# Turning the rows of the later steps by DMA over 16-bit planes in a GRU, ternary layer and mixture-of-experts kernel

## The chip, the cores and the metric

The kernel runs on one core of a Trainium2 chip. The metric is the device time of one launch in microseconds (us), lower is better; it is given as the median of several runs. The engines are called TensorE (PE in the profile; its weight loads are PEld), VectorE (DVE), ScalarE (ACT), GpSimd (POOL) and SyncE (SP, which issues DMAs). SBUF is the on-chip memory of 128 partitions, PSUM the accumulators that TensorE writes to.

## The reference, cut to what matters

The input is 128 sequences of 64 steps of 512 values (x: 128 x 64 x 512, float32) and a start state for each sequence (cond: 128 x 512). What is computed:

```
# block 0
h = cond
for t in 0..63:                       # GRU cell
    gi, gh = x[:, t] @ W_ih + b_ih, h @ W_hh + b_hh
    r = sigmoid(gi_r + gh_r);  z = sigmoid(gi_z + gh_z)
    n = tanh(gi_n + r * gh_n)
    h = (1 - z) * n + z * h
    hs[:, t] = h
x = x + hs @ ternary(weight).T * scale + bias
# block 1
c = causal depthwise convolution of x along the steps, 128 taps a channel = cond, + b
scores = softmax(c @ gate_w.T)        # 64 experts, the best 6 of each token
y = sum over the token's experts, at most 64 tokens an expert:
        score * (silu(c @ w_gate[e]) * (c @ w_up[e])) @ w_down[e]
x = x + y + (silu(c @ sw_gate) * (c @ sw_up)) @ sw_down      # the shared expert
```

The tokens are the 8192 pairs of sequence and step. The change touches the part between the convolution and the shared expert, and the very first loads.

## The kernel before

**Stages.** In the trace of before the GRU runs from 0 to about 1217 us, the convolution to about 1280, the shared expert with the routing (scores and the choice of the six experts) from 1280 to about 1758 as blocks i = 0 to 7, and the routed experts, with the other half of the shared expert's blocks laid among them, from there to the end. The program is written as one Python function for a framework that orders the instructions of each engine by itself from their dependencies; each engine then runs its own list in order, and waits at an instruction until what it needs is there. Where the program says `tc.issue_after` or `behind`, the order is set by hand.

**Rows and turned rows.** The convolution leaves its result in SBUF as `hid(t)`, one tile of 128 x 512 float32 for each of the 64 steps: 128 sequences on the partitions, 512 values along them. The tiles of the steps 0 to 31 and 32 to 63 are two buffers. The products need the 512 values on the partitions instead. So each step is *turned*: `turn(t)` (L1117 to L1129) transposes its four 128 x 128 parts on TensorE into one bank of PSUM (`pst`, L1128), and VectorE copies that bank back over `hid(t)` (L1138). Before that the rows, as they are, go to the table `tab` in device memory (`put_rows`, L1232, SP's queue), from which the routed experts later gather them. The turned rows of the steps from 32 on are also stored to `xts` (L1144, SP's queue), because the memory of `hid` is given to the experts' weights after block 7; they come back by the load at L1293.

**Blocks and routing.** A block is four steps (NB = 4), so there are NI = 16, and block i has steps 4i to 4i + 3. The loop `for i in range(NI // 2)` handles blocks 0 to 7 of the shared expert by `shared(i)`, a generator of 44 pieces, and draws from a second generator, `routing`, between the pieces. While block i's shared expert runs, `route` turns and scores blocks 2i + 1 and 2i + 2: eight turns at the start (one for each piece drawn), one group of logits (`lg`, L1152), and then for each of the two blocks the softmax, the score store to `tab` (L1196, SP's queue, two DMAs), and the choice of the best six. The tile `sc` that holds the scores is one buffer: the second block's scores overwrite the first's.

**The shared expert in a block.** Five chunks of seven products each (`winograd`, L824, into the banks psx, psw, psz and y), then two halves of the down product. A bank is one buffer (y has two), so TensorE goes on with a bank only when ScalarE or VectorE has taken its content out (L853 to L871); the evictions come one to three products before the bank is needed again. Sums of parts of the block's rows are kept in the memory of block i - 2 (`sums_space`), whose steps are done with by then.

**Finished blocks.** A finished block's rows are added to the output by four accumulating DMAs on GpSimd's queue (`add_shared`, L1106).

**The start.** Loads on SP's queue: the turned input of step 0 (`load_xt`, L256, 256 KB), then the GRU's input weights in halves of 512 KB (`load_halves` calls `load_rows`, L108). TensorE does some warm-up matmuls (L326) and then the first product (psy<-rawi,xp, L336).

Of the kernel before, what the change touches and what calls it, by code (L numbers as in the profile page):

```python
# [9 lines left out]
BF16 = mybir.dt.bfloat16  # L10
I32 = mybir.dt.int32
U8 = mybir.dt.uint8
F32R = mybir.dt.float32r
AF = mybir.ActivationFunctionType
ALU = mybir.AluOpType
# [4 lines left out]
P = 128  # L20
B = 128
T = 64
D = 512
# [24 lines left out]
def adaln_ffn_kernel(  # L48
# [57 lines left out]
    def load_rows(dst, src):  # L106

        return nc.sync.dma_start(out=dst, in_=src.rearrange("(k p) n -> p k n", p=P))  # L108
# [102 lines left out]
    with (  # L211
# [79 lines left out]
        def repeated(dst, row):  # L291
            nc.sync.dma_start(out=dst, in_=row.partition_broadcast(P))

        def load_halves(dst, src):
            for k in range(2):
                load_rows(dst[:, k * HK : (k + 1) * HK], src[k * HD : (k + 1) * HD])

        h = el0.tile([P, D], F32, name="h")
        bh = {0: io0.tile([P, D], F32, name="xn"), 1: el0.tile([P, D], F32, name="n")}

        load_xt(0, nc.sync)
        load_halves(raw_i[0], w_ih[:, cols[0]])
        load_halves(raw_i[2], w_ih[:, cols[2]])
        nc.sync.dma_start(out=h, in_=cond)
        load_xt(1, nc.sync)
        load_halves(raw_i[1], w_ih[:, cols[1]])
        load_rows(raw_h[0], w_hh[:, cols[0]])
        repeated(br, b_ih[cols[0]])
        repeated(bh[0], b_hh[cols[0]])
# [365 lines left out]
    def hid(t):  # L675
        return hids[t // TH][:, t % TH, :]
# [432 lines left out]
    with (  # L1109
        tc.tile_pool(name="sm", bufs=1) as sm,  # L1110
        tc.tile_pool(name="ps_t1", bufs=2, space=PSUM) as ps_t1,
        tc.tile_pool(name="ps_l", bufs=1, space=PSUM) as ps_l,
    ):

        sc = sm.tile([P, NB, NE + 2], F32, name="sc")  # L1117
        nc.gpsimd.memset(sc[:, :, NE:], -1.0)

        def turn(t):  # L1120

            if t in (2, 3):
                ps = ps_y.tile([P, D], F32, name="y")
            else:
                ps = ps_t1.tile([P, D], F32, name="pst1")
            ps = ps.rearrange("p (k b) -> p k b", k=KD)
            for k in range(KD):
                last = nc.tensor.transpose(ps[:, k, :], hid(t)[:, k * P : (k + 1) * P], ident)  # L1128
            return ps, last  # L1129

        def route(its, turned={}):


            for i in its:
                for t in range(i * NB, i * NB + NB):
                    ps = turned[t] if t in turned else turn(t)[0]
                    with behind(marks, t in turned):
                        copied = nc.vector.tensor_copy(  # L1138
                            hid(t).rearrange("p (k b) -> p k b", k=KD), ps
                        )  # L1140
                    if t == NB - 1:
                        marks.append(copied)
                    if t >= TH:
                        nc.sync.dma_start(out=xts[t - TH], in_=hid(t))  # L1144
                    yield


            lg = ps_l.tile([P, 2, 2, P], F32, name="lg")
            for n, i in enumerate(its):
                for k in range(KD):  # L1150
                    for h_ in range(2):
                        nc.tensor.matmul(  # L1152
                            lg[h_ * NE : (h_ + 1) * NE, n],
                            gw[:, k, :],
                            rows_of(i)[:, 2 * h_ : 2 * h_ + 2, k * P : (k + 1) * P],
                            start=(k == 0),
                            stop=(k == KD - 1),
                        )

            def logits(n):  # L1160
                ls = sh.tile([P, QT], F32, name="g2").rearrange("p (j b) -> p j b", j=2)
                nc.scalar.copy(ls, lg[:, n])
                return ls

            ls = logits(0)
            yield
            for n, i in enumerate(its):
                if len(its) == 1:
                    lgT = ps_l.tile([P, 2, 2, P], F32, name="lg")[:, 0]
                else:  # L1170
                    lgT = ps_t1.tile([P, D], F32, name="pst1")[:, :QT].rearrange(
                        "p (j b) -> p j b", j=2
                    )
                for j in range(2):
                    nc.tensor.transpose(lgT[:, j], ls[:, j, :], ident)

                lgT = lgT.rearrange("p j (h e) -> p (j h) e", h=2)
                nmax = sm.tile([P, NB], F32, name="nmax")
                nc.vector.tensor_reduce(nmax, lgT, AX.X, ALU.max)
                scn = sc[:, :, :NE]  # L1180
                nc.vector.tensor_tensor(
                    scn, lgT, nmax.unsqueeze(2).to_broadcast([P, NB, NE]), ALU.subtract
                )
                nc.scalar.activation(scn, scn, AF.Exp)
                yield
                ssum = sm.tile([P, NB], F32, name="ssum")
                nc.vector.tensor_reduce(ssum, scn, AX.X, ALU.add)
                nc.vector.reciprocal(ssum, ssum)
                nc.vector.tensor_tensor(
                    scn, scn, ssum.unsqueeze(2).to_broadcast([P, NB, NE]), ALU.mult  # L1190
                )
                yield
                top = sm.tile([P, NB, 8], F32, name="top")
                rep = sm.tile([P, NB, NE + 2], F32, name="rep")
                for a in range(2):
                    nc.sync.dma_start(  # L1196
                        out=tab_t[i * NB + 2 * a : i * NB + 2 * a + 2, :, D:].rearrange(
                            "t b e -> b t e"
                        ),
                        in_=sc[:, a::2, :NE],  # L1200
                    )
                for r in range(NB):
                    nc.vector.max(top[:, r], sc[:, r, :NE])
                nc.vector.memset(top[:, :, TOPK:], -1.0)
                if n + 1 < len(its):
                    ls = logits(n + 1)
                yield
                for j in range(NB):
                    t, r = i * NB + j, 2 * (j % 2) + j // 2
                    nc.vector.match_replace(rep[:, r], top[:, r], sc[:, r], -5.0)  # L1210
                    if t == 0:
                        nc.vector.tensor_scalar(
                            cum[:, t, :], rep[:, r, :NE], -5.0, None, ALU.is_equal
                        )
                    else:
                        nc.vector.scalar_tensor_tensor(
                            cum[:, t, :],
                            rep[:, r, :NE],
                            -5.0,
                            cum[:, t - 1, :],  # L1220
                            ALU.is_equal,
                            ALU.add,
                        )
                    if j % 2:
                        yield

        def put_rows(i):
            if i < NI:

                with tc.issue_after(loaded.ins):  # L1230
                    for t in range(i * NB, i * NB + NB):
                        (nc.gpsimd if i == 1 else nc.sync).dma_start(  # L1232
                            out=tab_t[t, :, :D], in_=hid(t)
                        )


        for i in range(1, 3):
            put_rows(i)
        load_rows(swd, sw_down[: full * P, :])
        for j in range(2):  # L1240
            nc.sync.dma_start(out=swdr[j * rest : (j + 1) * rest, :], in_=sw_down[full * P :, :])

        ahead = route([0])
        for _ in range(NB):
            next(ahead)

        with tc.issue_after(marks[-1].ins):
            marks.append(prepare_shared(0))
        second = {}
        for t in (NB, NB + 1):  # L1250
            second[t], last = turn(t)
        with tc.issue_after(last.ins):
            next(ahead)
        for i in range(NI // 2):
            put_rows(2 * i + 3)
            put_rows(2 * i + 4)

            def routing():
                if i == 0:
                    yield from ahead  # L1260
                its = [r for r in (2 * i + 1, 2 * i + 2) if r < NI]
                yield from route(its, second if i == 0 else {})

            routing_ = routing()
            done = 0
            for n, _ in enumerate(shared(i)):
                if done * PIECES <= n * 20:
                    with behind(products or marks, i == 0):
                        next(routing_, None)
                    done += 1  # L1270
            for _ in routing_:
                pass
            add_shared(i)
    first.close()
# [390 lines left out]
```

## Time and profile before

| what | value |
|---|---|
| median of 3 runs | 2451.47 us (2448.66 to 2453.61) |
| the profiled execution | 2452.42 us, span 2450.7 us |
| TensorE busy | 2436.9 us, 99% of the span |
| VectorE, ScalarE, GpSimd busy | 1546.5, 463.1, 445.8 us |
| start of the blocks 3, 4, 5, 6, 7, 8 of the shared expert | 1467.5, 1527.0, 1586.5, 1646.0, 1705.5, 1761.6 us |
| in block 4 (59.5 us): TensorE, VectorE, ScalarE, GpSimd busy | 59.5, 37.56, 14.37, 3.46 us |
| turns on TensorE | 64 steps, four transposes each |
| mean granted clock of TensorE | 0.999 |

All times are in us from the start of the span unless they are marked ns. In a line of a timeline the columns are start, duration, engine, source line, operation, written tile <- read tiles, shapes and count, and in brackets the idle time before it and what ended it. Durations of instructions that follow each other on one engine overlap a little, so that the distance of two starts, called the pitch here, is what an instruction costs its engine. SPq and POOLq stand for the queues that issue DMAs; a DMA lands when its data is there.

### The profile page before, as it was taken

What the parts mean: (1) busy time and instruction counts of PE and PEld (TensorE: products, weight loads), DVE (VectorE), ACT (ScalarE), POOL (GpSimd) and SP (SyncE); (2) the same over time, 40 slices, a digit from 0 to 9 for tenths busy, and PEclk for the clock granted to TensorE, in tenths of its full rate; (3) what the DMA queues carried; (4) which work ended last, traced back from release to release, by engine and by line L of the source; (5) the groups of instructions that cost most, each with busy time, mean ns of one, the idle gap of its engine ahead of it and who ended that gap; (6) DMA issues with size and microseconds to landing.
All of it is one profiled execution on the core that took longest, in us unless ns stands there. A gap on an engine that the chain in (4) does not pass through costs nothing.

```text
span 2450.7 us, 32124 instructions
## 1 busy us (share of the span) xinstructions
PE 2436.9 (99%) x12317; PEld 1883.7 (77%) x12317; DVE 1546.5 (63%) x3073; ACT 463.1 (19%) x847; POOL 445.8 (18%) x468
## 2 busy tenths in 40 slices
PE   9999999999999999999999999999999999999999
PEld 5888888888888888888896688888876666666667
DVE  8877777777777776777686566666653433343344
ACT  5211111111111111111122222222211111111111
POOL 1122221122112112211220000000012222222220
PEclk9999999999999999999999999999999999999999
DMA  5244443333232223222497112222468999899962
GB/s 183 68 95 81 82 80 63 61 69 65 56 61 56 56 56 62 56 52 52 142 343 270 24 23 44 62 59 61 116 174 287 300 290 312 267 330 293 283 175 52
DMA packets 464456, 322.33 MB, mean 132 GB/s; under 512 B 316592, under 2 KB 384176, under 8 KB 462128
## 3 DMA queue, kind: packets, MB, share of 16 engines
q1 hardware_dynamic: 435408, 246.34, 35.6%
q0 software_dynamic: 28896, 73.95, 13.5%
q8 instruction: 97, 1.59, 0.3%
q14 instruction: 55, 0.45, 0.1%
HBM read 233.44 MB, written 92.03 MB: 133 GB/s over the span
## 4 chain that ended last, share of the span: by engine, by line
PE 98%; DMA 1%; DVE 0%; issue 0%; ACT 0%; SPq 0%; POOL 0%; DVEq 0%; ACTq 0%
PE psa L336 9%; PE psx L336 9%; PE psw L336 9%; PE psx L824 8%; PE psw L824 8%; PE psz L824 8%; PE psy L336 5%; PE psb L336 5%; PE psz L336 5%; PE psf L336 5%; PE y L824 4%; PE py L1550 3%; PE pg L1524 3%; PE pu L1524 3%; PE y L1001 2%; PE psc L193 2%
## 5 line engine op out<-in xcount | busy, mean ns | idle before, releaser
L1534 DVE SCALAR_TENSOR_TENSOR a<-a,rw,pu 128x352 f32<-128x352 f32 x32 | 18.6, 580 | 213.4 <-PE pu L1524 213.4
L354 DVE SCALAR_TENSOR_TENSOR xs<-xl,xcut 128x512 fp32r<-128x512 f32 x63 | 103.6, 1644 | 66.0 <-POOL xl L353 66.0
L347 DVE TENSOR_SCALAR hcut<-pst 128x512 int32<-128x512 int32 x63 | 43.5, 691 | 129.8 <-PE pst L419 127.6
L1106 POOL DMA_DIRECT2D out_dram<-hid x32 | 27.7, 1006 | 449.6 <-issue 333.5
L353 POOL TENSOR_TENSOR xl<-xp,xcut 128x512 fp32r<-128x512 f32 x60 | 82.8, 1380 | 145.2 <-PE psa L336 145.1
L488 ACT ACTIVATE rz<-rz 128x512 f32<-128x512 f32 x64 | 40.5, 633 | 336.1 <-DVE rz L487 336.1
L433 ACT CAST hh<-hcut 128x512 fp32r<-128x512 f32 x61 | 37.9, 622 | 325.0 <-DVE hcut L347 325.0
L271 POOL DMA_DIRECT2D q<-in_x_dram x36 | 19.3, 537 | 409.7 <-DMA out_dram<-q 313.4
L1550 PE MATMUL py<-wd,aeT 128*64 128x512 f32 (+1 forms) x384 | 88.8, 597 | 0.0
L1524 PE MATMUL pg<-wg,xeT 128*64 128x352 f32 x512 | 81.2, 459 | 0.0
L1524 PE MATMUL pu<-wu,xeT 128*64 128x352 f32 x512 | 81.2, 459 | 0.0
L1561 POOL DMA_INDIRECT out_dram<-ys,idxp x32 | 47.0, 1469 | 183.4 <-DMA out_dram<-ys,idxo 103.7
L1561 POOL DMA_INDIRECT out_dram<-ys,idxo x32 | 45.0, 1407 | 174.3 <-DMA out_dram<-ys,idxp 168.1
L336 PE MATMUL psa<-wih1h,xh 128*128 128x512 f32 x252 | 74.5, 416 | 0.0
L271 POOL DMA_DIRECT2D xn<-in_x_dram x28 | 15.0, 536 | 319.1 <-DMA out_dram<-xn 258.3
L1524 PEld LDWEIGHTS pg<-wg,xeT 128*64 128x64 f32 x512 | 36.3, 136 | 47.4 <-issue 47.4
L864 ACT ACTIVATE g<-psx 128x256 f32<-128x256 f32 x80 | 30.7, 384 | 217.5 <-DVE aT L871 158.5
L501 ACT ACTIVATE n<-n 128x512 f32<-128x512 f32 x64 | 40.5, 633 | 163.3 <-DVE n L500 160.9
L336 PE MATMUL psw<-wih2h,xh 128*128 128x512 f32 x252 | 68.7, 394 | 0.0
L336 PE MATMUL psw<-wih2l,xl 128*128 128x512 f32 x252 | 68.5, 392 | 0.0
L336 PE MATMUL psa<-wih1l,xl 128*128 128x512 f32 x252 | 68.2, 392 | 0.0
L336 PE MATMUL psb<-wih1s,xs 128*128 128x512 f32 x252 | 68.1, 392 | 0.0
(429 smaller groups left out, 6170.2 us busy)
## 6 DMA issues: line engine op xcount, KB each, us to landing
wg<-in_w_gate_dram SPq DMA_DIRECT2D x64, 704.0 KB, 12.5
wu<-in_w_up_dram SPq DMA_DIRECT2D x64, 704.0 KB, 12.8
wd<-in_w_down_dram SPq DMA_DIRECT2D x64, 512.0 KB, 10.5
xc<-x1c SPq DMA_DIRECT2D x32, 512.0 KB, 6.8
xp<-in_xT_dram POOLq DMA_DIRECT2D x62, 256.0 KB, 2.9
tab<-hid SPq DMA_DIRECT2D x56, 256.0 KB, 4.3
wd<-in_w_down_dram SPq DMA_DIRECT2D x64, 192.0 KB, 10.7
q<-in_x_dram POOLq DMA_DIRECT2D x36, 256.0 KB, 2.9
```

Source lines behind the costliest of these rows:

```text
L193: i = nc.tensor.matmul(ps[rows, j].rearrange("p h (u t) -> p h u t", u=2), xcs[sl % NCB][:, rows, g * 4 + j], tzs[sl % NCB][:, :, :, g * 4 ...
L336: i = nc.tensor.matmul(ps, lhs[:, k, :], rhs[:, k, :], start=start and k == 0, stop=stop and k == KD - 1, skip_group_check=True,)
L347: return nc.vector.tensor_scalar(dst.bitcast(I32), src.bitcast(I32), LOW, None, ALU.bitwise_and)
L353: i = engine.tensor_sub(lo, full, cut)
L354: nc.vector.scalar_tensor_tensor(mix, lo.bitcast(F32), -SPLIT, cut, ALU.mult, ALU.add)
L488: nc.scalar.activation(r, r, AF.Sigmoid)
L501: nc.scalar.activation(n, n, AF.Tanh)
L824: i = nc.tensor.matmul(ps.rearrange("p (j b) -> p j b", b=P) if len(r.shape) == 3 else ps, lhs(k), r, start=(first and k == 0), stop=(k == ...
L1001: nc.tensor.matmul(gu.rearrange("p (j b) -> p j b", b=P), swr[:, k].rearrange("p w n -> p (w n)"), rows[:, k], start=(k == 0), stop=(k == ...
L1524: nc.tensor.matmul(acc[halves[j]], self.xeT[:, k, halves[j]], self.ws[j][which][:, k, :], start=(k == 0), stop=(k == KD - 1),)
L1550: nc.tensor.matmul(py[halves[j]], self.aeT[:n, c, halves[j]], self.ws[j][2][:n, c, :], start=(c == 0), stop=(c == len(ech) - 1),)
L1561: nc.gpsimd.indirect_dma_start(out=out, out_offset=bass.IndirectOffsetOnAxis(ap=(idxp[:CAP] if j == 0 else idxo)[:, q : q + 1], axis=0), i ...
```

## The change

Three edits.

The steps from 36 on (blocks 9 to 15) are no longer turned by TensorE. In their place a new generator, `turn_away(i)`, runs beside the shared expert's blocks from i = 3 on and turns the steps of the blocks 2i + 3 and 2i + 4, one block of the loop earlier than `route` needs them. For each step ScalarE copies the lower and the upper 16 bits of the 512 words into two planes in a flat buffer (two copies), a transposing DMA on SP's queue turns both planes at once into a second buffer (eight 128 x 128 parts of 16-bit elements), and VectorE copies the two turned planes back over `hid(t)`, each into its half of the words (two copies, two steps later in program order: LAG). These are the four portions of a step, one to each piece of the shared expert. The buffers are the tiles of steps 0 to 7, whose content is no longer needed: two flat and three turned ones for i = 3, three and five after that. `route` then skips its turns for these blocks and begins with the logits.

For the same steps the stores to `xts` go to GpSimd's queue, and so do the score stores of the blocks from 9 on.

At the start, the input of step 0 is loaded on ScalarE's queue, and the first block of the GRU's input weights in four quarters instead of two halves.

```diff
-        load_xt(0, nc.sync)
-        load_halves(raw_i[0], w_ih[:, cols[0]])
-        load_halves(raw_i[2], w_ih[:, cols[2]])
+        load_xt(0, nc.scalar)
+        load_parts(raw_i[0], w_ih[:, cols[0]], KD)
+        load_parts(raw_i[2], w_ih[:, cols[2]])
...
+        AWAY = 3
+        LAG = 2
+        def plane(t, n):
+            return hid(t).bitcast(U16)[:, n * D : (n + 1) * D]
+        def word_halves(t):
+            return hid(t).bitcast(U16).rearrange("p (d h) -> p d h", h=2)
+        def turn_away(i):
+            steps = [
+                t for r in (2 * i + 3, 2 * i + 4) if r < NI for t in range(r * NB, r * NB + NB)
+            ]
+            flat_at, turned_at = (
+                ((0, 1), (2, 3, 7)) if i == AWAY else ((0, 1, 2), (3, 4, 5, 6, 7))
+            )
+            for n in range(len(steps) + LAG if steps else 0):
+                for w in range(2):
+                    if n < len(steps):
+                        at = flat_at[n % len(flat_at)]
+                        nc.scalar.copy(plane(at, w), word_halves(steps[n])[:, :, w])
+                        if w:
+                            nc.sync.dma_start_transpose(
+                                out=hid(turned_at[n % len(turned_at)])
+                                .bitcast(U16)
+                                .rearrange("p (m b) -> p m b", b=P),
+                                in_=hid(at).bitcast(U16),
+                            )
+                    yield
+                    if n >= LAG:
+                        t, at = steps[n - LAG], turned_at[(n - LAG) % len(turned_at)]
+                        nc.vector.tensor_copy(word_halves(t)[:, :, w], plane(at, w))
+                        if w and t >= TH:
+                            nc.gpsimd.dma_start(out=xts[t - TH], in_=hid(t))
+                    yield
...
         def route(its, turned={}):
-            for i in its:
+            apart = its[0] > 2 * AWAY + 2
+            for i in its if not apart else ():
...
-                    nc.sync.dma_start(
+                    (nc.gpsimd if apart else nc.sync).dma_start(
                         out=tab_t[i * NB + 2 * a : i * NB + 2 * a + 2, :, D:].rearrange(
...
+            turning = turn_away(i) if i >= AWAY else iter(())
             done = 0
             for n, _ in enumerate(shared(i)):
                 if done * PIECES <= n * 20:
                     with behind(products or marks, i == 0):
                         next(routing_, None)
                     done += 1
+                next(turning, None)
             for _ in routing_:
+                pass
+            for _ in turning:
                 pass
             add_shared(i)
```

More of the change, by code (lines that the diff above doesn't have):

```diff
@@ L12 @@
 U8 = mybir.dt.uint8
+U16 = mybir.dt.uint16
 F32R = mybir.dt.float32r
@@ L292, in repeated, with load_parts @@
             nc.sync.dma_start(out=dst, in_=row.partition_broadcast(P))
-        def load_halves(dst, src):
-            for k in range(2):
-                load_rows(dst[:, k * HK : (k + 1) * HK], src[k * HD : (k + 1) * HD])
+        def load_parts(dst, src, n=2):
+            for k in range(n):
+                load_rows(
+                    dst[:, k * KD // n : (k + 1) * KD // n], src[k * D // n : (k + 1) * D // n]
+                )
         h = el0.tile([P, D], F32, name="h")
         bh = {0: io0.tile([P, D], F32, name="xn"), 1: el0.tile([P, D], F32, name="n")}
-        load_xt(0, nc.sync)
-        load_halves(raw_i[0], w_ih[:, cols[0]])
-        load_halves(raw_i[2], w_ih[:, cols[2]])
+        load_xt(0, nc.scalar)
+        load_parts(raw_i[0], w_ih[:, cols[0]], KD)
+        load_parts(raw_i[2], w_ih[:, cols[2]])
         nc.sync.dma_start(out=h, in_=cond)
         load_xt(1, nc.sync)
-        load_halves(raw_i[1], w_ih[:, cols[1]])
+        load_parts(raw_i[1], w_ih[:, cols[1]])
         load_rows(raw_h[0], w_hh[:, cols[0]])
@@ L1129, in turn @@
             return ps, last
+        AWAY = 3
[22 more added lines that the diff above has]
+                                in_=hid(at).bitcast(U16),
+                            )
+                    yield
[5 more added lines that the diff above has]
+                    yield
         def route(its, turned={}):
-            for i in its:
+            apart = its[0] > 2 * AWAY + 2
+            for i in its if not apart else ():
                 for t in range(i * NB, i * NB + NB):
```

## The prediction

> **What bounds the kernel now.** I read the page's busy shares and chain first. Times below come from one profiled execution: 2452.42 us for a span of 2450.7, that is 0.95 above the median of 2451.47; differences are summed against the span and then taken from the median.
>
> ```profile
> PE 2436.9 (99%) x12317; PEld 1883.7 (77%) x12317; DVE 1546.5 (63%) x3073; ACT 463.1 (19%) x847; POOL 445.8 (18%) x468
> ...
> PE 98%; DMA 1%; DVE 0%; issue 0%; ACT 0%; SPq 0%; POOL 0%; DVEq 0%; ACTq 0%
> ```
>
> TensorE is the path: what it no longer does is worth its full pitch, as long as no other engine, VectorE first, comes late. The timeline of TensorE at the start of the shared block i = 5 prices the work removed:
>
> ```profile
> 1590.02 0.60 PE L1128 MATMUL pst<-ident,hid 128*128 128x128 f32 x4
> 1590.46 1.03 PE L824 MATMUL psx<-hid,sw0first 128*128 128x256 f32 x4
> ...
> 1593.05 0.60 PE L1128 MATMUL pst<-ident,hid 128*128 128x128 f32 x4
> 1593.49 1.03 PE L824 MATMUL psx<-hid,sw0first 128*128 128x256 f32 x4
> ```
>
> Start to start, one step's turn costs 0.44 us (the next one 0.43). Then the windows. The changed kernel's compiled order (order only, no times) puts the new copies and turns into two stretches. The first 12 steps stand from the end of block i = 2's gate part to early in block 3, which is 1448 to 1484 in this trace. The last 16 stand from the end of block 3's gate part to the second chunk of block 4, 1507 to 1541; 10 or 11 of these cluster at the seam, 1511 to 1532. Columns: PE, PEld, DVE, ACT, POOL busy, clock, DMA share, GB/s.
>
> ```profile
> 1448.00:1484.00 36.00, 36.00 (x176) 29.20 (x175) 23.16 (x65) 6.17 (x14) 3.46 (x4) 1.00 0.26 41
> 1507.00:1541.00 34.00, 34.00 (x166) 27.41 (x165) 21.69 (x64) 6.29 (x13) 3.47 (x4) 1.00 0.33 66
> 1511.00:1532.00 21.00, 21.00 (x97) 15.99 (x96) 11.58 (x38) 2.03 (x5) 3.47 (x4) 1.00 0.35 48
> ```
>
> TensorE is full in all three; VectorE has 12.8, 12.3 and 9.4 us free, ScalarE 29.8, 27.7 and 19.0. Last, the DMA issues (KB each, median us from issue to landing), as no turn by DMA stands in this trace:
>
> ```profile
> x1c<-q SPq DMA_DIRECT2D x36, 256.0 KB, 4.5
> ...
> xts<-hid SPq DMA_DIRECT2D x32, 256.0 KB, 2.0
> ...
> tab<-sc SPq DMA_DIRECT2D x32, 64.0 KB, 1.7
> ...
> tab<-xl POOLq DMA_DIRECT2D x4, 32.0 KB, 5.8
> ```
>
> **The change, part by part.**
>
> *Removed: 28 turns on TensorE* (steps 36 to 63; blocks 4, 5 and 6 lose eight each, block 7 four). 28 x 0.435 = 12.2 us, all on the path. VectorE also loses 28 copies out of PSUM (L1138, 0.69 each, 19.3 us), but in blocks 4 to 7, mostly after the stretches that fill up.
>
> *Added on ScalarE: 56 plane copies* of 128x512. The row for such a copy is 0.62 (xh<-xcut, L377): 24 in the first stretch are 14.9 us against 29.8 free, 32 in the second 19.8 against 27.7. Priced at nothing; the cover is ScalarE's idle time. Were it gone, an eviction would wait one copy, 0.62, and the first reads of psx have some 2 us (the products that lie between) to spare.
>
> *Added on VectorE: 56 word copies*, 16-bit, reading rows and writing every second half word. No such copy is in the trace. Bounds: the SBUF-to-SBUF pass xcut<-xp, 0.42 for 128x512, pitch 0.38; and the copy out of PSUM, 0.69. I take 0.38, because source and destination both lie in SBUF as in xcut. At the seam 23 of them stand between the same neighbours: 23 x 0.38 = 8.7 of 9.4 free us. VectorE just fits, with nothing to spare.
>
> *Added: 28 turns on SP's queue, and waits on them.* ScalarE waits for a turn before it refills that flat buffer (two buffers for the first eight steps, then three), VectorE before the word copies; both run in order, so the evictions that TensorE needs are queued behind. What counts is landing time L against the distance the order leaves. I laid the compiled orders of all engines side by side with row durations (done for before, this gives 60.1 us for a block, the profile 59.5). Example: between the third turn's issue and its word copy VectorE has the three sums of 128x512 that open a block, pitch 0.72, so 2.2 us. ScalarE's distances are often shorter, but it has idle time to absorb its waits; VectorE's are below 2.9 in some 18 of the 28, mostly between 2.2 and 2.8. So L up to about 2.6 costs nothing, and past that about 18 turns each push the path by the excess: 18 x (L - 2.6).
> L is bounded by xts<-hid, 2.0 (same tiles, same size, same queue, same blocks) and x1c<-q, 4.5 (the same bytes in 4096 pieces of 64). The compiled turn works in tiles of 16 rows by 128 16-bit elements, so 256-byte pieces, 1024 of them; tab<-sc moves 256 such pieces in 1.7. By pieces between those two: 1.7 + 768/3840 x 2.8 = 2.3. Turns often issue in pairs, and behind another one waits 0.66 (the pitch of 27 row stores in 17.81 us on SP), half the time: 0.3; a wait sees a landing 0.1 late. L = 2.7, cost 1.8, rounded to 2.0. A gain is excluded: a wait frees nothing.
>
> The Trainium skill speaks against the change: VectorE: DVE Perf Modes, The three transpose paths, puts a 128x128 16-bit transpose at 390 ns on TensorE and 1309 ns by crossbar DMA, and advises TensorE where PSUM will do. Eight such blocks in sequence would be an estimated 10.5 us a step, and the sum would end near 2580 (18 x 7.9 in place of 2.0). DMA: Bandwidth & Descriptors, Latency and other measured facts, gives an effective 261 GB/s for such DMAs, an estimated 1.0 us for 256 KB, which would leave the sum as it is; no run here shows either yet.
>
> *Moved: 28 row stores (xts) to GpSimd's queue.* GpSimd pays 0.87 each (L1106), 24.4 us, and is busy 3.46 of 59.5 per block; their reader (the row load at 1720) is far off. Nothing. They stand ahead of the add stores, which have a block's time.
>
> *Moved: 14 score stores to GpSimd's queue.* VectorE must not overwrite the scores before they are read out: in block 3 they are ready at 1500.70, and the next write starts at 1506.33, 5.6 us later. Two issues, 0.87 each, and a landing of 5.8 (tab<-xl) make up to 6.7, so 1.1 late, in the three blocks with two halves. Bounds 0 (SP's 1.7 fits) and 3.3; I take 1.0, since VectorE has slack again by then. Behind that write stand the evictions of the chunk.
>
> *SP's queue.* The turns pass nothing urgent: the row stores are issued by 1341, weights only from 1721. Block 3's own score stores stand behind turns; they have 5.6 us for 1.7.
>
> *The first block in quarters, xp on ScalarE's queue.* TensorE idles 0.90 at 4.48, until the first half (512 KB) lands 4.0 after its issue:
>
> ```profile
> 1.26 3.99 DMA rawi<-in_w_ih_dram
> 5.25 0.14 issue
> 5.38 6.11 PE psy L336 x8
> ```
>
> A 256 KB quarter, issued first, lands before the warm-up matmuls end (2.9 for xp<-in_xT), so 0.9 goes. Bounds 0 (the four quarters share the engines, DMA 92% busy) to 3.3 (TensorE's passes run at a pitch of 0.86 until about 10.2, then at 0.43; were they at 0.43 from 5.4 on, 2.4 more would go). I take 0.9, the idle row itself.
>
> Sum: -12.2 - 0.9 + 2.0 + 1.0 = -10.1; 2451.47 - 10.1 = 2441.4.
>
> **The rivals.** A measurement of this kernel tells some 0.2%, 4.9 us, from no change.
>
> *A, the forecast:* L below 3.0, word copies near 0.38. 2437 (no waits, start gain kept whole, -14) to 2446.5. For it: xts<-hid at 2.0 in the same place, DMA share only 0.25 to 0.35. Chance 0.56.
>
> *B, the gain is eaten:* word copies at 0.69: the seam needs 11.58 + 23 x 0.69 = 27.5 of 21 us, so 6.5 late: 2441.4 + 6.5 = 2447.9; or L of 3.0 to 3.5, 5 to 14 instead of 2. The time lands within 4.9 of before, 2446.6 to 2456.4. For it: the seam has under 1 us free. Against: SBUF-to-SBUF rows are 0.42. Chance 0.20.
>
> *C, slower: the turn's landing.* At the seam and in the first stretch VectorE stands in order behind turns. With L = 4.5, as x1c<-q, 18 x 1.9 = 34.2 instead of 2.0: 2441.4 + 32.2 = 2473.6. It decides from 2.6 + 12.1/18 = 3.3 on (break-even), and passes 0.2% at 3.5. For it: tab<-hid, whole rows of the same tiles, took a median of 4.3 with many in flight; the turns also come many at a time. Against: the ring of three buffers never has more than three in flight. Chance 0.22.
>
> *D, the DMA does not turn in pieces* but element by element: 435408 packets took 35.6% of 16 engines' 2450.7 us, 32 ns each; 131072 elements are 262 us a step on 16 engines, and 28 steps end near 9.8 ms. Against: the compiled turn names 16x128 tiles. Chance 0.02.
>
> **How the numbers follow.** Faster is A, 0.56; same is B, 0.20; slower is C and D, 0.24. The time is A's, 2441.4. The range runs from 2437 (0.04 of A below) to C with L = 4.1: 18 x 1.5 = 27, so 2466; C's upper part and D, 0.14, are beyond. A alone has 2437 to 2446.5.
>
> **What would show it.** Right: no turn on TensorE from block 4 on; blocks 4 to 6 near 56 us, block 3 and 4 perhaps 1 or 2 more; turns landing in 2 to 3 us; VectorE's waits on them under 5 us in all; first product near 4.5. Wrong: VectorE or ScalarE waiting on hid turns for tens of us with TensorE behind (C); word copies of 0.69 and VectorE full from 1511 on (B); a turn that holds its queue for 5 us or more.

## The result, and the profile after

The changed kernel takes 2473.11 us (median of 4 runs, 2472.34 to 2474.9) against 2451.81 of the kernel before beside it: a ratio of 1.0089, 95% interval 1.0072 to 1.0107, or 21.3 us more. The forecast was 2441.4. The time is near that of rival C, 2473.6. The profiled execution took 2474.9 us, its span 2473.2.

The page of the changed kernel, busy shares and chain of waits:

```profile
PE 2432.5 (98%) x12205; PEld 1875.8 (76%) x12205; DVE 1545.4 (62%) x3101; ACT 493.7 (20%) x903; POOL 475.6 (19%) x510
...
PE 93%; DMA 4%; DVE 1%; ACT 0%; issue 0%; POOL 0%; SPq 0%; DVEq 0%; ACTq 0%; POOLq 0%
```

TensorE runs 112 instructions fewer (28 turns of 4) and saves only 4.4 us of busy time. The chain, 98% TensorE before, now has 4% of DMA in it. The answer for the line that issues the turns (L1159) says which DMA; the numbers after the colon are ns of the issue, min/median/max, the last ones us to landing:

```profile
L1159 SPq DMA_TRANSPOSE hid<-hid x28: 1232/1271/3949, 1449.9 to 1577.6; - x28
...
  ACT hid L1157: 55.0, 18
  DVE hid L1168: 44.9, 15
...
DMA to landing us min/median/max: 3.0/4.8/7.8
```

A turn lands 4.8 us after its issue, never under 3.0, where the sum had 2.7. ScalarE stood 55.0 us before turns, which I had priced at nothing, and VectorE 44.9, where I had written "under 5 us in all". The blocks' windows, cut at their first product (L1004; columns as in the prediction), blocks i = 2 to 5:

```profile
1405.55:1467.32 61.77, 59.76 (x306) 48.36 (x305) 37.51 (x114) 19.40 (x37) 4.56 (x6) 1.00 0.24 43
1467.32:1546.63 79.31, 65.40 (x307) 50.79 (x305) 46.01 (x141) 30.52 (x58) 12.26 (x18) 0.91 0.58 118
1546.63:1618.19 71.56, 60.79 (x274) 46.97 (x272) 40.13 (x130) 24.32 (x47) 14.05 (x21) 0.90 0.56 109
1618.19:1674.15 55.96, 55.96 (x274) 45.34 (x273) 32.56 (x106) 14.44 (x29) 6.41 (x8) 1.00 0.16 24
```

Block 5 is what was hoped for: 55.96 us against 59.50, 3.54 for eight turns, 0.44 each. Blocks 2, 3 and 4 should have been 59.5, 59.5 and 56.0 and are 61.8, 79.3 and 71.6, a loss of 37.7 us. 26.7 of it is TensorE idle (2.0, 13.9 and 10.8, length less busy time). The rest is TensorE busy for longer with the same work, 5.9 us more in block 3 and 4.8 in block 4. The clock column says why: 0.91 and 0.90. The timelines of VectorE and ScalarE around 1485, and under them that of TensorE from 1477 to 1492, show both parts (in brackets the idle time ahead and what ended it):

```profile
1484.34 1.50 DVE L1168 COPY hid<-hid 128x512 uint16<-128x512 uint16 x4 [6.04 <-DMA hid<-hid]
1485.73 0.41 DVE L858 TENSOR_TENSOR u<-u,y 128x256 f32<-128x256 f32 x1
```
```profile
1484.32 0.62 ACT L1157 COPY hid<-hid 128x512 uint16<-128x512 uint16 x1 [6.25 <-DMA hid<-hid]
1484.85 0.36 ACT L856 COPY u<-psx 128x256 f32<-128x256 f32 x1
```
```profile
1477.75 2.07 PE L827 MATMUL psw<-hid,sw1first 128*128 128x256 f32 x4 [4.57 <-DVE hid L1026]
...
1485.26 2.07 PE L827 MATMUL psx<-hid,sw0first 128*128 128x256 f32 x4 [4.58 <-ACT u L856]
1487.13 1.91 PE L827 MATMUL psw<-hid,st 128*128 128x256 f32 x4
...
1491.07 1.03 PE L827 MATMUL psx<-hid,sw 128*128 128x256 f32 x4
```

VectorE stands 6.04 us before word copies; behind them in its list is the eviction L858 that TensorE's banks wait for, and on ScalarE, after 6.25 us, the eviction L856 stands behind a plane copy in the same way. After the idle stretch four matmuls take 2.07 in place of 1.03, until about 1491. The waits of TensorE, in us, times and longest, say whom it waited for in the three blocks:

```profile
PE psx L827 <- ACT u L856: 9.0, 2, 4.6
...
PE pst L1217 <- ACT g L1204: 4.8, 1, 4.8
PE psw L827 <- DVE hid L1026: 4.6, 1, 4.6
```

All in all TensorE stood 14.0 us behind ScalarE and 12.7 behind VectorE, the 26.7 of above.

### The profile page after: what moved, and what is told of

Read it like the earlier page. It is cut to its first block, busy times and chain, and to the rows that moved or that the text cites. A ratio compares the mean times of both kernels' runs of the same rounds, so it can differ in the third digit from the quotient of the medians.

```text
span 2473.2 us, 32065 instructions
## 1 busy us (share of the span) xinstructions
PE 2432.5 (98%) x12205; PEld 1875.8 (76%) x12205; DVE 1545.4 (62%) x3101; ACT 493.7 (20%) x903; POOL 475.6 (19%) x510
## 3 DMA queue, kind: packets, MB, share of 16 engines
q0 software_dynamic: 31584, 82.21, 13.7%
## 4 chain that ended last, share of the span: by engine, by line
PE 93%; DMA 4%; DVE 1%; ACT 0%; issue 0%; POOL 0%; SPq 0%; DVEq 0%; ACTq 0%; POOLq 0%
PE psa L339 9%; PE psw L339 9%; PE psx L339 9%; PE psx L827 7%; PE psz L827 7%; PE psw L827 7%; PE psb L339 5%; PE psz L339 5%; PE psf L339 5%; PE psy L339 5%; PE y L827 4%; PE py L1596 3%; PE pg L1570 3%; PE pu L1570 3%; DMA hid<-hid 3%; PE y L1004 2%
## 5 line engine op out<-in xcount | busy, mean ns | idle before, releaser
L272 POOL DMA_DIRECT2D xn<-in_x_dram x28 | 15.1, 538 | 319.1 <-DMA out_dram<-xn 266.2
L858 DVE TENSOR_TENSOR u<-u,y 128x256 f32<-128x256 f32 x80 | 33.5, 419 | 61.0 <-PE y L827 58.9
L339 PE MATMUL psy<-wih0s,xs 128*128 128x512 f32 x252 | 68.2, 392 | 0.5 <-DVE rz L487 0.5
## 6 DMA issues: line engine op xcount, KB each, us to landing
wd<-in_w_down_dram SPq DMA_DIRECT2D x64, 192.0 KB, 10.5
```

Of the source, the lines that this page charges most:

```text
L339: i = nc.tensor.matmul(ps, lhs[:, k, :], rhs[:, k, :], start=start and k == 0, stop=stop and k == KD - 1, skip_group_check=True,)
```

## The experiments

**Theory landing:** a turn takes longer to land than the compiled order leaves between its issue and the copies that need it, and evictions are queued behind those copies. **Rivals:** the copies' work itself; GpSimd's queue, which got the row stores; turns that land late only because of crowding. In the comparisons below the floor is before less 14.5: 12.2 for the turns and 2.3 for the start; what lies above it is called the loss. By that measure the changed kernel's loss is 35.8.

**The start alone**, on the kernel before:

```diff
-        load_xt(0, nc.sync)
-        load_halves(raw_i[0], w_ih[:, cols[0]])
+        load_xt(0, nc.scalar)
+        load_parts(raw_i[0], w_ih[:, cols[0]], KD)
```

> The kernel before with the start's edit alone (first loads on ScalarE's queue, first block of input weights in four quarters). Between the two profiles the first block of the shared expert began 2.3 us earlier after the change (1282.7 against 1285.0), and nothing but the start had changed up to there. If that is the start's worth, this kernel takes 2.3 us less than before, some 2449. The prediction had put it at 0.9, so 2450.6. Were it 0, the 2.3 would come from the difference between two executions.

2449.85 against 2452.14: 2.3 us less, ratio 0.9992 (0.9983 to 1.0001), so the size is as expected though the interval just touches no change. Little of it is the idle row that I priced: the first product starts at 4.92 in this run's profile and at 5.12 in that of the changed kernel, instead of 5.38, as it now waits for xp on ScalarE's queue. The rest comes along with differences of the clock. TensorE's window from 41.1 to 47.8, first of the kernel before, then of the changed one, then of this run:

```profile
41.10:47.80 6.70, 6.03 (x9) 2.52 (x8) 4.65 (x10) 3.81 (x7) 0.55 (x1) 0.50 0.33 97
```
```profile
41.10:47.80 6.70, 6.38 (x20) 3.14 (x19) 6.70 (x14) 4.77 (x9) 0.56 (x1) 1.00 0.29 96
```
```profile
41.10:47.80 6.70, 6.70 (x16) 3.26 (x15) 5.45 (x12) 3.67 (x7) 0.56 (x1) 0.84 0.32 98
```

Before, TensorE ran there at a granted clock of 0.50 and did 9 instructions; in the changed kernel it has 1.00 and does 20, and the pass psy<-rawh,xn takes 3.60 us after 6.52. In this run, with the same start as the changed kernel, the clock was at 0.50 from 39.83 to 43.24, and the pass takes 4.23; its very first pass, psy<-rawi,xp, takes 4.07 us where it took 6.11 before and 5.78 in the changed kernel. So two profiles of the same start save the time in different places. What in the edit keeps the clock up longer is not shown.

**A plain DMA in place of the turn:**

```diff
-                            nc.sync.dma_start_transpose(
-                                out=hid(turned_at[n % len(turned_at)]).bitcast(U16).rearrange("p (m b) -> p m b", b=P),
-                                in_=hid(at).bitcast(U16),
-                            )
+                            nc.sync.dma_start(out=hid(turned_at[n % len(turned_at)]).bitcast(U16),
+                                              in_=hid(at).bitcast(U16))
```

> The changed kernel with a plain DMA of the same 256 KB from the flat buffer to the second one in place of each turning DMA, on the same queue (the rows of the steps from 36 on stay unturned). All copies by ScalarE and VectorE, all row, score and add stores stay, and the order is nearly the same. Theory landing: the time is lost because a turn lands 4.8 us (median) after its issue where the order leaves 2.6; the stores of the same bytes landed in 2.0 (before) to 2.9 us (after), so at most 18 x 0.3 = 5 us of waits stay: 2437 to 2444. Rival work (the 56 + 56 copies overload ScalarE and VectorE): all of it stays, 2473. Rival GpSimd's queue (row stores delay the add stores, VectorE waited 10.3 us for one): most of it stays, above 2460.

2456.39, ratio 1.0018 (1.0009 to 1.0027), 4.3 above before: a loss of 18.8, half of it gone and half not. None of the three numbers was met. The waits on the DMA are still 58.0 us (ScalarE 34.1, VectorE 23.9), so a plain DMA, too, lands too late in this order. One point of my expectation was misread: VectorE's 10.3 us for an add store is no part of the change, the profile of before has the same wait with 10.7 us, ended at 1343, some 100 us ahead of the first turn. The DMA view of the first transfer by itself (busy share in tenths of the 16 DMA engines, then GB/s, in 40 slots of 0.085 us), from 1449.8 to 1453.2; the changed kernel (issue at 1449.91):

```profile
DMA  0289930300000000279999999999999510000000
GB/s 0 57 208 235 202 70 0 96 0 0 0 0 0 0 0 0 42 160 217 226 226 223 193 238 190 226 196 193 232 190 199 115 21 0 0 0 0 0 0 0
...
hid<-hid SPq DMA_TRANSPOSE x1, 3.2
```

and the one with the plain DMA (issue at 1450.10):

```profile
DMA  9401799500300000059999999500000000000000
GB/s 202 97 3 27 184 241 199 115 6 0 96 0 0 0 0 0 0 217 386 361 410 386 386 386 361 193 0 0 0 0 0 0 0 0 0 0 0 0 0 0
```

The bursts on the left are score stores. The turn keeps all 16 engines busy for 1.4 us at some 210 GB/s, the plain DMA for 0.75 at 386. A turn's issue takes SP's queue 1.24 to 1.27 us (median) against 0.47, and its first byte moves 1.2 us after the issue begins. This one lands after 3.2 us; the shortest landing of all is 3.0.

**Both copies paced:** held behind evictions of the shared expert, so that the order keeps the pace of the generator.

```diff
+    paced = {}                       # latest eviction of a chunk on each engine
...
-                nc.scalar.copy(self.u2, ps)
+                paced["act"] = nc.scalar.copy(self.u2, ps)
-                self.summed = add(self.u3, ps, self.u2)
+                self.summed = paced["dve"] = add(self.u3, ps, self.u2)
...
+                        with tc.issue_after(paced["act"].ins):
                             nc.scalar.copy(plane(at, w), word_halves(steps[n])[:, :, w])
...
+                        with tc.issue_after(paced["dve"].ins):
                             nc.vector.tensor_copy(word_halves(t)[:, :, w], plane(at, w))
```

> The changed kernel with each plane copy and each word copy held behind the latest eviction of the shared expert on its engine in program order, so that the compiled order has 16 plane copies and 16 word copies in each of the blocks 3 to 5 and 8 in block 6, and between a turn and its word copies lie two steps, some 10 us. The same 28 turns, copies and stores. Theory landing: even a landing of 7.8 us, the longest seen, is covered; what is left is the 12.2 us of turns that TensorE no longer does and the start: 2451.5 - 12.2 - 2.3 + 1 for small waits = 2438 (2436 to 2444). Rival work: VectorE and ScalarE have the same copies, but spread: 4 x 4 us of 56, so this rival too would expect a gain if bunching alone were its cause, but VectorE's waits on turns would have to be replaced by late evictions; 2445 to 2455. Rival GpSimd's queue: row stores still stand ahead of the add stores, a loss of some 10 us stays: 2448.

2442.4 against 2452.14, ratio 0.9964 (0.995 to 0.9978): 9.7 us faster than before, and some 31 faster than the changed kernel with the same turns, copies and stores. It is the fastest of the kernels here that compute the whole result. The line of the turns, now with five waits, 3.5 us in all:

```profile
L1161 SPq DMA_TRANSPOSE hid<-hid x28: 1232/1238/2689, 1470.8 to 1661.4; - x28
...
  DVE hid L1171: 3.5, 5
```

and its blocks 3 to 6:

```profile
1464.84:1524.52 59.68, 59.68 (x307) 48.42 (x305) 41.72 (x130) 22.39 (x45) 7.98 (x12) 1.00 0.49 111
1524.52:1581.25 56.73, 56.62 (x274) 45.11 (x273) 37.01 (x122) 22.31 (x45) 11.04 (x16) 1.00 0.48 98
1581.25:1639.90 58.65, 56.89 (x274) 45.09 (x272) 36.80 (x122) 22.44 (x45) 11.00 (x16) 1.00 0.51 95
1639.90:1696.50 56.60, 56.49 (x275) 45.20 (x273) 34.91 (x114) 17.83 (x36) 8.64 (x12) 1.00 0.31 61
```

TensorE is nearly full again at a clock of 1.00. What is left above 59.5, 56.0, 56.0 and 56.0 is 4.3 us, 2.7 of it in block 5. The longest wait of VectorE for a turn, 2.26 us, stands there, and right behind it the only wait of TensorE in these blocks, 1.65 us ahead of the product at 1604.44, for an eviction by VectorE.

**Only the plane copies paced** (the last added line of that diff, which holds the word copies back, taken out again):

> As the paced kernel, but only the plane copies on ScalarE are held back; the word copies on VectorE stand where the compiler puts them, close behind the turns. The turns are spread over the blocks 3 to 6, so they do not crowd each other. Theory landing by distance: VectorE still stands before turns that have not landed; with the landing at 3.0 (the shortest seen) 28 x 0.4 to 0.6 = 11 to 17 us of the gain go, 2445 to 2455; if it is still 4.8, some 2470. Rival crowding (the landing is long only because turns come many at a time): landing 3.0 or less and a time near the paced kernel's, 2440 or less.

2454.7, ratio 1.0012 (1.0003 to 1.0021): a loss of 17.1, against 4.8 with both paced. It lies in the range of the theory by distance (2445 to 2455). VectorE stands before turns for 25.6 us in 19 waits. Spreading the turns alone does not do it; the word copies have to stand further off.

**Without the eight add stores of the blocks 2 and 3:**

```diff
+            if i not in (2, 3):
                 add_shared(i)
```

> The changed kernel without the eight add stores of the blocks 2 and 3 (the outputs of these blocks lack the shared expert), the compiled order otherwise the same. They are issued by GpSimd at 1460 to 1475 and at 1536 to 1551, in the middle of the turns, and land in a median of 5.4 us. By the start distances of the blocks the changed kernel loses 37.7 us in the blocks 2, 3 and 4 against 59.5, 59.5 and 56.0. Theory crowding (a turn lands in 3.0 by itself and 4.8 only because stores take the DMA engines): the landing's median falls to some 3.8, the loss to 18 x 1.2 = 22, the time to 2457. Theory turn alone (4.8 is what turns bunched like this take): the time stays above 2468.

2464.42, ratio 1.0048 (1.0032 to 1.0064): the loss goes from 35.8 to 26.5. It falls between the two theories. ScalarE and VectorE wait 45.3 and 32.6 us instead of 55.0 and 44.9.

**Without the DMA:**

```diff
-                            nc.sync.dma_start_transpose(...)
+                            pass
...
-                ((0, 1), (2, 3, 7)) if i == AWAY else ((0, 1, 2), (3, 4, 5, 6, 7))
+                ((0, 1, 2, 3, 7), ()) if i == AWAY else ((0, 1, 2, 3, 4, 5, 6, 7), ())
...
-                        t, at = steps[n - LAG], turned_at[(n - LAG) % len(turned_at)]
+                        t, at = steps[n - LAG], flat_at[(n - LAG) % len(flat_at)]
```

> The changed kernel without the turning DMAs: the word copies read the flat buffers themselves (the rows of the steps from 36 on stay unturned), which the eight free tiles all serve as. The 56 plane copies, 56 word copies and all stores stay; the compiler bunches the word copies more than in the changed kernel (17 before and 17 after the start of block 4). Theory landing: without a landing to wait for nothing of the loss stays but what the bunches cost by themselves, 2437 to 2442. Rival work: in the kernel with the plain DMA 19 of 37.7 us of loss stayed; if that is the copies' work and not the plain DMA's landing, it stays here too: 2455 or more.

2440.78, ratio 0.9954 (0.9938 to 0.997): a loss of 2.9. The blocks 3 and 4 are 59.61 and 55.95 long, so the 112 copies, with 34 word copies bunched around one block's start, cost about 0.1 us there. Block 2 is where time is lost, 64.40 against 59.5: there a plane copy waits 5.90 us for an add store (out_dram<-hid), and the clock is at 0.50 for 3.4 us. The rival "work" is out.

**Without any of GpSimd's stores in the stretches** (the add stores of the blocks 2 and 3 left out, the row stores of the turned steps after block 5):

```diff
-                            nc.gpsimd.dma_start(out=xts[t - TH], in_=hid(t))
+                            late.append(t)
...
-            add_shared(i)
+            if i not in (2, 3):
+                added = add_shared(i)
+            if i == 5:
+                with tc.issue_after(added.ins):
+                    for t in late:
+                        nc.gpsimd.dma_start(out=xts[t - TH], in_=hid(t))
```

> As the kernel without the eight add stores, and the row stores of the turned steps issued only after block 5, so that in the stretches of the turns no store of GpSimd's queue is left. Theory crowding: turns land near 3.2, the loss is 18 x 0.6 = 11, the time 2452.1 - 12.2 - 2.3 + 11 = 2449. Theory turn alone: above 2465. If turns crowd each other (up to three in flight at 1.2 us of all 16 engines each), it ends between.

2453.01, ratio 1.0003 (0.9993 to 1.0012): a loss of 15.1. The row stores are worth 11.4 more than the add stores' 9.3, and crowding by stores makes up 20.7 of 35.8. The other 15.1 stays with no store of GpSimd's queue in the stretches: 32.0 and 22.8 us of waits on turns are left.

**Finer pacing** (the other evictions of a chunk as places too):

> The paced kernel with every eviction of a chunk as a place to hold copies behind, so that VectorE's word copies stand one or two at a time between evictions (four at a time in the paced kernel, whose blocks 3 to 6 still lose 4.3 us by their start distances, 2.7 of it in block 5). If these bunches are what is left, 2438 to 2440; if it is the landing of turns issued two in a row, no change from the paced kernel: 2442.

2442.62, ratio 0.9962 (0.9947 to 0.9976): no change from the paced kernel, so the bunches of four word copies are not what is left. That leaves the other theory, turns that land late, which the wait in block 5 speaks for; no run takes it away by itself.

**Paced, one step apart** (`LAG = 1`):

> The paced kernel with the word copies one step behind the turns instead of two (LAG 1): the same spread, the same copies and stores, but some 4 to 5 us between a turn's issue and its word copies instead of 10. Theory landing by distance: a turn with nothing beside it takes 3.0 to 3.2, one that is issued in a pair or beside add stores 5 to 8, so only some of the 28 are late: 2445 to 2450, between the paced kernel (2442.4) and the one with free word copies (2454.7). Rival (not the distance but the bunches of word copies on VectorE make the difference between these two): as the paced kernel, 2442.

2452.76, ratio 1.0001 (0.9992 to 1.001): a loss of 15.1, outside the 2445 to 2450 of the theory and near the kernel with free word copies. My distance was wrong: in this trace VectorE is done with what stands ahead of a turn's first word copy 2.0 to 5.6 us after the turn's issue, 3.2 in the median, not 4 to 5; in the paced kernel 3.4 to 10.3 us, 5.4 in the median, not 10. Read with these distances the run fits; the answer for the line of its turns:

```profile
  DVE hid L1171: 22.4, 15
...
DMA to landing us min/median/max: 3.0/3.5/5.6
```

A median landing of 3.5 against a median distance of 3.2 makes VectorE wait 15 times, 1.5 each. The bunches of word copies are like the paced kernel's, so this rival is out.

**Paced, row stores after block 5:**

> The paced kernel with the row stores of the turned steps issued only after block 5 (all add stores stay). In the unpaced kernel taking these stores out of the stretches of the turns was worth 11 us; where the distance covers the landing they should be worth next to nothing: theory landing by distance 2440 to 2443, no change from the paced kernel's 2442.4. If their crowding costs by itself, about 2438.

2453.83, ratio 1.0006 (0.9997 to 1.0015): 11 us slower than the paced kernel, which neither theory had. The blocks 3 to 5 are 59.68, 56.73 and 58.59 long, within 0.1 of the paced kernel's: there the row stores are worth nothing, as the theory had it. Block 6 is the difference, 68.56 against 56.60; its window:

```profile
1640.57:1709.13 68.56, 59.51 (x274) 46.41 (x273) 35.30 (x114) 17.93 (x36) 21.63 (x36) 0.95 0.63 142
```

and the answer for the line of the turns:

```profile
  DVE hid L1173: 13.1, 8
...
DMA to landing us min/median/max: 3.0/3.1/15.4
```

GpSimd now issues 24 of its row stores between 1644 and 1666, into the last four turns: these took 11.5 to 15.4 us to land, more than the 10.3 of the paced kernel's longest distance, and TensorE idled 4.8 us ahead of 1670. By accident this is the clearest view of crowding: the median turn takes 3.1.

## Why the prediction was wrong, point by point

**The step that failed is the landing time, L = 2.7.** It measured 4.8, and rival C, which put L at 4.5 with a chance of 0.22, was the case that came. That C's sum, 2473.6, meets the time is in part luck. Its slope, 18 x (L - 2.6), counts VectorE's waits alone; with 4.8 it gives 39.6, near the 37.7 that the blocks lost. But of those 37.7 TensorE stood only 12.7 behind VectorE, 14.0 behind ScalarE and 11.0 are matmuls that took longer; neither of the last two is in the sum. Three things were missing in "2.3 by pieces + 0.3 + 0.1":

- *The turn by itself.* 3.0 to 3.2, not 2.3: SP's queue is busy 1.27 us with its issue, and 1.4 us of transfer follow. I interpolated between plain DMAs by the number of pieces, and a turning DMA is none of them. Break-even was put at 3.3, so by that slope even an undisturbed turn would have used up most of the gain. The kernel without GpSimd's stores, 0.6 from no change, agrees, though some of its turns still kept VectorE until 4.1 to 4.6 us after their issue.
- *Stores on the same 16 engines.* "Nothing" for the row stores moved to GpSimd's queue looked at the queue and the reader only. Each row store comes right behind a step's word copies, so beside the next turn, and the add stores of the blocks 2 and 3 start at 1460 and 1536 in the changed kernel. From 1461.5 to 1465.5 the DMA share is 1.03 and a turn issued at 1462.04 has to wait. I had read the share as a mean, 0.26 to 0.35, over 21 to 36 us; in the profile of before the window 1461 to 1466 has 0.69, and would have told it. Taking both kinds of stores out gave 20.7 of 35.8.
- *Turns beside turns.* "Half of them behind another one, 0.66": a turn behind another waits up to 1.27 us for its issue. Once issued, the second need not be slower. In the kernel without GpSimd's stores two turns issued 1.3 us apart (at 1540.25 and 1541.57) ended VectorE's waits 3.3 us after their issue each (at 1543.52 and 1544.91). The ring of three buffers did not protect: ScalarE, which refills the flat ones, waited 55.0 us.

**"ScalarE has idle time to absorb its waits" was wrong too.** Plane copies wait in order before evictions, and that cost TensorE no less than VectorE's waits did: 14.0 us, in three stretches of 4.83, 4.58 and 4.38 for the most part.

**Not in the sum: the clock.** Idle TensorE costs more than the idle time. Windows of the changed kernel just ahead of and in the first slow stretch:

```profile
1463.50:1477.10 13.60, 9.69 (x42) 6.17 (x40) 4.31 (x12) 3.33 (x7) 2.88 (x4) 1.00 0.84 144
1477.12:1490.78 13.66, 8.44 (x23) 6.55 (x24) 6.21 (x15) 5.71 (x13) 1.65 (x3) 0.50 0.81 144
```

There are two such stretches of 13.7 us at 0.50, from 1477 and from 1559; each begins within an idle stretch of TensorE (4.57 and 4.83 us long), and they are most of the 10.7 us by which TensorE is busy for longer in the blocks 3 and 4. The Trainium skill has a rule for this (TensorE: Matmul & The Clock Gate, HAM oscillation: no idle gaps of TensorE above some 3.4 us, or the clock goes down to half). The two gaps here agree with it. Other gaps are shorter than the rule has it and were followed by a slow stretch all the same: 2.23 and 0.67 us in the kernel before at 41 us, 2.09 in the kernel without the DMA at 1413. And gaps of 2.49 at 38 us and 3.21 at 1540 in the changed kernel brought none, so the length of one gap does not decide it here.

**What held.** The turns removed: 3.54 per eight, as priced (0.44). Plane copies: 617 ns for 620. Word copies: 449 ns one by one, and four in a row 1.50, a pitch near 0.35 for 0.38, so rival B's 0.69 was not seen, and in the run without the DMA the copies cost about 0.1 us in the blocks 3 and 4. (In B, "5 to 14 instead of 2" is what comes on top of the 2; the slope itself gives 7.2 and 16.2.) The score stores: VectorE waited 0.3 for them where I took 1.0. The add stores' delay behind row stores, priced at nothing, showed no wait of its own; their packets did. The start: 2.3 instead of 0.9, of which the first product's earlier start is 0.3 to 0.5 and the rest goes with the clock. Rival D did not come.

**The two estimates from figures of the Trainium skill** lay on either side. The 10.5 us a step from 1309 ns a block (VectorE: DVE Perf Modes, The three transpose paths) was too long, as the eight blocks of a turn share one burst of 1.4 us. The 1.0 us from 261 GB/s (DMA: Bandwidth & Descriptors, Latency and other measured facts) was too short even for that burst, and leaves out the 1.2 us before it.

The mechanism is shown from both ends. The same turns give 2473.1 in the order that the compiler chose, 2452.8 paced with a median distance of 3.2 us, and 2442.4 with 5.4; without the DMA the same copies give 2440.8. Two things stay open: how the 15.1 us without GpSimd's stores divide between a turn's own 3.0 and the turns that took longer, and what the last 4 us of the paced kernel are, beyond the wait in block 5. As the kernels without stores also differ by a few places of copies, their shares hold for this order of taking away only.

## What to carry to other kernels

A transfer that is put between two copies of in-order engines is priced by its landing against the distance that the compiled order leaves, and everything queued behind the copy pays: if the landing is not in the trace, take the slowest near row for the forecast, or lay the order so that twice that would fit. A generator that yields in step with the main work does not pace anything by itself when the instructions are reordered by dependencies; hold them behind instructions of the main work, on the producer's and on the consumer's engine: pacing the producer alone gave 2454.7, both 2442.4. Of two waiting engines, price both: the one with idle time, ScalarE here, held TensorE up as much as the busy one. And moving a DMA to another queue moves its issue, not its bytes.

## What the runs showed of the hardware that was not expected

- A turning DMA of 256 KB between SBUF tiles occupies SP's queue for 1.23 to 1.27 us and all 16 DMA engines for 1.4 us (some 210 GB/s), and lands 3.0 us after its issue at best; a plain one of the same bytes 0.47 us and 0.75 us (386 GB/s).
- Beside stores the same turn took 4.8 (median) and up to 7.8 us, and 11.5 to 15.4 beside a run of row stores.
- Within idle stretches of TensorE of 4.6 and 4.8 us the granted clock fell to 0.50 and stayed there for 13.7 us each time; at 41 us of the kernel before it was 0.50 over a window of 6.7 us, after gaps of only 2.2 and 0.7, while a gap of 3.21 us in the changed kernel at 1540 brought no slow stretch.
